# Layer 3's marks for experts: more of them at the MLPs' last products, at the attention's projections and at its first transposes

## The chip, the cores and the metric

The kernel runs on one core of a Trainium2 chip. The metric is the device time of one execution in microseconds (us), the median of several runs. TensorE is called PE, VectorE DVE, ScalarE ACT, GpSimd POOL and SyncE SP, as in the profile.

## The reference

The reference is a chain of four layers on x, 8 sequences of 256 tokens with 128 features, all in float32. Each layer is a macaron: half a feed-forward part, an attention part, half a feed-forward part again, each behind a layer norm and added to x. Only layer 3 matters here:

```python
x = x + 0.5 * _L3_ffn_ref(_layernorm(x), ...)
x = x + _L3_attn_ref(_layernorm(x), ...)
x = x + 0.5 * _L3_ffn_ref(_layernorm(x), ...)

def _L3_ffn_ref(x, ...):            # attention within a sequence, then eight dense experts
    x = x + softmax(q k^T * scale) v @ Wo + bo
    gates = softmax(x @ Wg + bg)
    hmid = relu(einsum('bsh,ehd->bsed', x, W1) + b1)      # 8 experts, 128 -> 512
    eout = einsum('bsed,edh->bseh', hmid, W2) + b2        # 512 -> 128
    return x + einsum('bse,bseh->bsh', gates, eout)

def _L3_attn_ref(x, ...):
    xm = mix(x); n = rms_norm(xm)
    value, gate = split(n @ in_proj)                      # causal convolution, silu
    Bm, Cm = xm @ B_proj, xm @ C_proj
    xm = xm + scale * ((scan(value, Bm, Cm) + D * value) * silu(gate) @ out_proj)
    xm = xm + scale * (relu(rms_norm(xm) @ fc)**2 @ proj)     # MLP "m"
    xa = mix(xm, x); n = rms_norm(xa)
    q, k, v = n @ q_w, n @ k_w, n @ v_w                   # 16 heads of 8, 4 of k and v; norms, rope
    xa = xa + scale * (softmax(causal q k^T) v @ o_w)
    return xa + scale * (relu(rms_norm(xa) @ a_fc)**2 @ a_proj)   # MLP "a"
```

## The kernel before

Tokens lie on the 128 partitions; x stays in SBUF as 16 tiles of 128 tokens by 128 features. After layer 0 the kernel works in two halves, `a` and `b`, of four sequences (1024 tokens) each. The stages of a half are numbered 0 to 11; layer 3 is 9 (`l3_ffn`), 10 (`l3_attn`) and 11 (`l3_ffn` again). `run` writes out an order in which a stage of one half is built beside the experts of the other: the experts of (b, 9) beside stage (a, 10), those of (a, 11) beside (b, 10), those of (b, 11) alone at the end.

An expert part is a loop over eight experts `e` and two groups `g` of 512 tokens (`l3_ffn`, lines 1595 to 1620). For each it makes four `ph` products (L1600), relu with bias into `hT` (three on ACT, L1608, the fourth on DVE, L1606), sixteen `po` products (L1612) and four updates of `x_res` on DVE (L1618). The weights of an expert come by `experts` (L943), in turn from SP's and ACT's queue, into three buffers; so a load waits for the expert three before it.

A scheduler of the framework sets the order of instructions on each engine; each engine then runs its queue in order. What ties the experts to the other half are marks. `step(inst, weight)` appends an instruction of the stage to a list, `weight` times. `keep_pace` picks for every `ph` an entry of that list and makes a dependency without a semaphore: the scheduler puts the `ph` behind that instruction, and nothing waits for it on the chip.

```python
    def step(self, inst, weight=1):
        self.steps += [inst.ins] * weight
    def keep_pace(self, inst, part):
        if self.pace:
            mark = self.pace[int(part * self.share * (self.marks or len(self.pace)))]
```

`part` is (2 * e + g) / 16. `share` is 0.8 (`EARLY`) for (b, 9) and 1.0 for (a, 11). So the place of a `ph` depends on the whole length of the list and on where its entries lie.

The marks of one stage 10 before, in the order of the list:

- `l3_scan`, the scan of four batches (sequences): 16 in each, at the products `sc` (L1752). A batch begins with `pv` (L1712), a convolution on DVE (L766, L768) and silu on ACT, transposes `pvt` (L1720), the gate `pg` (L1730), then `pbc` (L1746), `sc`, `y` (L1766), and ends with `yT` on DVE and POOL (L1772, L1775) and `po` (L1779).
- `l3_mlp` "m": `rms` (L1629 to L1635: square on ACT, sum, root on ACT, reciprocal L238, scaling L1634, transposes L231), then for two groups four `ph` (L1659, a mark each), relu on ACT, square on POOL and DVE (L1665), sixteen `po` (L1669): 8 marks.
- `blend` (L1867 to L1871), and in `l3_gqa` the setup (`attn_setup`: casts, four issues on ACT L544), `rms` and the projections `qkv` (L1802, 2 marks each): 16 marks.
- `attn_batches`: for each of four batches `prepare` (rotations on DVE and POOL, L1840 to L1845), `attn_stack` (a split of q and k in three bf16 parts, L573 to L576, 24 transposes `tpb` L593 in eight groups of three, evictions `sT`, and a trip through DRAM: `l_parts` L600 from SP for q and from ACT for k, then `qs` and `ks` L601 from SP), one batch later the maxima (`attn_max`, L617 to L621) and three later the mixing (`attn_mix`, L653 to L700). Maxima and mixing have 8 marks per batch each: 64.
- `l3_mlp` "a": 8 marks.

Together 160.

Of the kernel before, what the change touches and what calls it, by code (L numbers as in the profile page):

```python
# [19 lines left out]
NT = T // P  # L20
# [145 lines left out]
class Chip:  # L166
# [411 lines left out]
    def attn_stack(self, a, b, q, k, pool, psum):  # L578


        nc = self.nc
        kv = a["kv"]
        n = 8 * kv
        sT = pool.tile([P, 2, 3, S], BF16, name="sT", tag="sT")
        qs = pool.tile([75, 16, S], BF16, name="qs", tag="qs", bufs=4)
        ks = a["ks"][b % 4]
        for side, (x, m, h, dst) in enumerate(((q, P, 16, qs), (k, n, kv, ks))):
            sp = pool.tile([P, 3, 2, m], BF16, name=f"sp{side}", tag=f"sp{side}")
            self.split3(pool, x, [sp[:, i] for i in range(3)], f"sp{side}")
            for t in range(2):  # L590
                ps = psum.tile([P, 3, P], BF16, name="tpb", tag="m")
                for i in range(3):
                    nc.tensor.transpose(ps[0:m, i, :], sp[:, i, t, :], a["ident_b"])  # L593
                at = (1 - t if side == 0 else t) * P
                self.evict(sT[0:m, side, :, at : at + P], ps[0:m])

            dr = self.tc.dram_tile([3, 3, m, S], BF16, name=f"l_parts{side}")
            for i in range(3):
                out = (dr[i], dr[:, i])[side]
                (nc.sync, nc.scalar)[side].dma_start(out.rearrange("s r t -> r s t"), sT[0:m, side])  # L600
            nc.sync.dma_start(  # L601
                dst[0:72].rearrange("r h t -> r (h t)"), dr.rearrange("i s (d h) t -> (i s d) (h t)", h=h)
            )
        return qs
# [272 lines left out]
class Half(Chip):  # L877
# [768 lines left out]
    def l3_mlp(self, xm, n, scale):  # L1646

        nc = self.nc
        with ExitStack() as ctx:
            pool = ctx.enter_context(self.sb("l3m"))  # L1650
            fc, proj = self.load(pool, f"l3a_{n}fc"), self.scaled(pool, f"{n}proj", scale)
            wk = ctx.enter_context(self.sb("l3mw", 2))
            psum = ctx.enter_context(self.ps("l3mps", 2))
            nT = self.rms(pool, psum, xm, "h")
            for g in range(self.T // 512):
                hT = wk.tile([P, 4, 512], F32, name="hT", tag="hT")
                for k in range(4):
                    ps = psum.tile([P, 512], F32, name="ph", tag="h")
                    mm = nc.tensor.matmul(  # L1659
                        ps, fc[:, k * P : (k + 1) * P], nT[:, 512 * g : 512 * g + 512], start=True, stop=True  # L1660
                    )
                    self.step(mm)
                    nc.scalar.activation(hT[:, k, :], ps, AF.Relu)
                    eng = (nc.gpsimd, nc.vector)[k % 2]
                    eng.tensor_tensor(hT[:, k, :], hT[:, k, :], hT[:, k, :], ALU.mult)  # L1665
                po = psum.tile([P, 4, D], F32, name="po", tag="o")
                for i in range(4):
                    for k in range(4):
                        nc.tensor.matmul(  # L1669
                            po[:, i, :], hT[:, k, i * P : (i + 1) * P], proj[:, k, :], start=(k == 0), stop=(k == 3)  # L1670
                        )
                xs = xm[:, 4 * g : 4 * g + 4, :]
                nc.vector.tensor_tensor(xs, xs, po, ALU.add)

# [110 lines left out]
    def l3_gqa(self, xa):  # L1785

        nc, NT = self.nc, self.NT
        with ExitStack() as ctx:
# [4 lines left out]
            a = self.attn_setup(one, 4, 1)  # L1793
# [3 lines left out]
            with self.sb("l3gn") as np_:  # L1797
                nT = self.rms(np_, psum, xa, "m")
                for g in range(0, NT, 2):
                    ps = psum.tile([P, 2, 192], F32, name="qkv", tag="m")  # L1800
                    for i in range(2):
                        mm = nc.tensor.matmul(  # L1802
                            ps[:, i, :], nT[:, (g + i) * P : (g + i + 1) * P], w["qkv"], start=True, stop=True
                        )
                        self.step(mm, 2)
                    self.evict(qk[:, g : g + 2], ps[:, :, 0:160])
                    nc.scalar.copy(v[:, g : g + 2].rearrange("p t h d -> p t (h d)"), ps[:, :, 160:192])
            part = lambda z, k: (z[:, :, 0:P], z[:, :, P:160])[k].rearrange("p t (d h) -> p t d h", d=8)
# [97 lines left out]
```

## Time and profile before

| | before |
|---|---|
| median of 5 runs | 2828.45 us (2823.78 to 2832.7) |
| the profiled execution, time | 2824.83 us |
| the profiled execution, span from first to last instruction | 2823.0 us |
| mean granted PE clock | 0.889 |
| PE / DVE / ACT / POOL busy | 83% / 57% / 36% / 11% |

The page of the profile lists the busy time of every engine, groups of instructions by line with their mean time, and the chain of work that ended last. Further views are cut to a stretch of time: a table of stretches (busy time, granted PE clock, share of DMA), a timeline of one engine (start, length, line, what is written from what, and in brackets the idle time before it with what ended it) and the waits. A float32 product shows as two rows, one for each of its two passes; a bf16 product as one.

In the profiled execution the scan's four batches of half a end at 1822.4, 1866.6, 1909.7 and 1952.9 us, those of half b at 2274.2, 2318.3, 2360.4 and 2406.4 (starts of L1779).

### The profile page before, as it was taken

The page shows a single profiled execution, that of the slowest core. Times are in us where ns is not written, and L with a number is a line of the kernel's source. Part 1 is how long each engine was busy: PE and PEld are TensorE (multiplying, and loading weights), DVE is VectorE, ACT ScalarE, POOL GpSimd, SP SyncE. Part 2 cuts the span into 40 slices and gives each one's busy share as a digit, 9 for nine tenths or more (in the row PEclk, how much of TensorE's full clock was granted, in tenths as well). Part 3 has the DMA queues.
Part 4 walks back from the last instruction along what each step waited for, and adds up shares of the span by engine and source line. Part 5 has one row for each costly group of instructions (what it writes and reads, how often), then busy time and mean ns, then how long its engine had stood idle before and what let it go on. Part 6 is the DMA issues. An engine that isn't in the chain of part 4 may idle for free. (4 is left out here: it accounts for less than half of the span.)

```text
span 2823.0 us, 42755 instructions
## 1 busy us (share of the span) xinstructions
PE 2334.3 (83%) x17346; PEld 1544.9 (55%) x17346; DVE 1597.6 (57%) x3704; ACT 1027.3 (36%) x1754; POOL 319.5 (11%) x441
## 2 busy tenths in 40 slices
PE   5794788579689979878797898999698798779999
PEld 3672455367454535545465555666455565546666
DVE  6536442753458888788558746444644643453422
ACT  1021333212349669335453335212235321223322
POOL 0372110037000000000000000001201000210000
PEclk8695889669799989979998899899899899889999
DMA  7134321513200000110011001000211000030100
GB/s 259 21 42 108 104 79 45 208 22 41 79 19 17 16 23 23 32 30 24 7 40 32 17 16 50 1 16 17 68 47 38 27 8 16 26 93 3 43 23 23
DMA packets 103027, 127.27 MB, mean 45 GB/s; under 512 B 15161, under 2 KB 84094, under 8 KB 97726
## 3 DMA queue, kind: packets, MB, share of 16 engines
q1 hardware_dynamic: 61706, 71.56, 8.6%
q10 hardware_dynamic: 28836, 43.28, 4.6%
q0 software_dynamic: 12288, 9.71, 2.5%
q8 instruction: 136, 2.23, 0.3%
q14 instruction: 61, 0.50, 0.1%
HBM read 96.84 MB, written 27.53 MB: 44 GB/s over the span
## 5 line engine op out<-in xcount | busy, mean ns | idle before, releaser
L1612 PEld LDWEIGHTS po<-w_e,hT 128*128 128x128 f32 x2048 | 260.6, 195 | 69.6 <-issue 43.9
L1612 PE MATMUL po<-w_e,hT 128*128 128x128 f32 x2048 | 283.3, 283 | 12.0 <-DVE hT L1606 7.7
L1600 PE MATMUL ph<-x2T,w_e 128*128 128x512 f32 x512 | 267.1, 625 | 7.0 <-ACT hT L1608 6.3
L1608 ACT ACTIVATE hT<-ph,w_l_cols 128x512 f32<-128x512 f32 x192 | 131.5, 686 | 310.0 <-PE ph L1600 306.1
L621 DVE TENSOR_REDUCE nm<-sc 128x3 f32<-128x384 f32 (+1 forms) x192 | 130.5, 689 | 127.6 <-PE sc L619 126.4
L1040 PEld LDWEIGHTS po<-w_e,hT 128*128 128x128 f32 x1024 | 136.1, 199 | 80.0 <-DVE hT L1033 34.5
L658 ACT ACTIVATE pr_e<-scT 128x384 f32<-128x384 f32 (+1 forms) x192 | 111.3, 597 | 171.0 <-PE scT L655 161.1
L1040 PE MATMUL po<-w_e,hT 128*128 128x128 f32 x1024 | 146.0, 287 | 17.4 <-DVE hT L1033 13.3
L1030 PE MATMUL pu<-xnT,w_e 128*128 128x512 f32 x256 | 136.3, 614 | 8.7 <-ACT gs L1032 8.7
L231 PE MATMUL tp<-c_ident,xn 128*128 128x128 f32 x208 | 53.6, 379 | 105.0 <-DVE xn L251 97.0
L1027 PE MATMUL pg<-xnT,w_e 128*128 128x512 f32 x256 | 136.0, 613 | 1.8 <-ACT gs L1032 1.1
L1618 DVE SCALAR_TENSOR_TENSOR x_res<-po,gt,x_res 128x128 f32<-128x128 f32 x256 | 80.0, 358 | 86.3 <-PE po L1612 85.8
L500 ACT ACTIVATE gs<-pg 128x512 f32<-128x512 f32 x64 | 38.2, 597 | 248.7 <-PE pg L495 231.8
L1600 PEld LDWEIGHTS ph<-x2T,w_e 128*128 128x128 f32 x512 | 84.8, 195 | 69.9 <-ACT hT L1608 35.4
L1033 DVE SCALAR_TENSOR_TENSOR hT<-pu,w_l_bias,gs 128x512 f32<-128x512 f32 x128 | 94.7, 744 | 48.2 <-PE pu L1030 46.5
L1032 ACT ACTIVATE gs<-pg,w_l_bias 128x512 f32<-128x512 f32 x128 | 87.2, 688 | 86.5 <-PE pg L1027 78.8
L668 PE MATMUL ctx<-pr_e,vz 128*32 128x256 f32 x512 | 107.3, 397 | 2.8 <-ACT pr_e L658 2.8
L1758 DVE TENSOR_TENSOR gw<-sc,dec 128x768 f32<-128x768 f32 x64 | 61.2, 957 | 82.8 <-PE sc L1752 82.3
L513 POOL DMA_INDIRECT l_acc<-eo,idx x64 | 101.9, 1592 | 33.9 <-issue 16.3
L231 PEld LDWEIGHTS tp<-c_ident,xn 128*128 128x128 f32 x208 | 34.0, 171 | 125.5 <-DVE xn L251 82.0
L617 PE MATMUL sc<-ks,qs 72*128 72x256 bf16 x256 | 76.2, 298 | 28.3 <-DMA ks<-l_parts 17.5
L1046 ACT ACTIVATE ys<-po,pr 128x128 f32<-128x128 f32 x256 | 73.3, 368 | 63.9 <-PE po L1040 63.2
(604 smaller groups left out, 4991.5 us busy)
## 6 DMA issues: line engine op xcount, KB each, us to landing
l_parts<-sT SPq DMA_DIRECT2D x48, 192.0 KB, 5.2
qs<-l_parts SPq DMA_DIRECT2D x16, 576.0 KB
w_l_wu<-in_l_wu ACTq DMA_DIRECT2D x8, 1024.0 KB
w_e<-in_l_e SPq DMA_DIRECT2D x16, 512.0 KB, 3.6
w_e<-in_l_e ACTq DMA_DIRECT2D x16, 512.0 KB, 4.2
w_e<-in_l_e SPq DMA_DIRECT2D x16, 384.0 KB, 3.3
w_e<-in_l_e ACTq DMA_DIRECT2D x16, 384.0 KB, 3.0
l_parts<-sT ACTq DMA_DIRECT2D x24, 192.0 KB, 4.2
```

The costliest lines, as they stand in the source:

```text
L231: self.held(self.nc.tensor.transpose(ps[:, i * P : (i + 1) * P], src_of(g + i), self.ident), "tensor")
L513: nc.gpsimd.indirect_dma_start(out=accs[h][:, :], out_offset=bass.IndirectOffsetOnAxis(ap=idx[:, j : j + 1], axis=0), in_=eo[:, h, :], in_ ...
L621: nc.vector.tensor_reduce(blocks[:, hp * pr : hp * pr + hp, :], sc[:, :, 0:384].rearrange("p h (k t) -> p h k t", t=P), AX.X, ALU.max, neg ...
L658: nc.scalar.activation(pe, sc[:, :, 0:384], AF.Exp, scale=float(1.0 / np.sqrt(np.float32(8.0))))
L668: nc.tensor.matmul(o, z, pe[:, 0:S], start=(j == 0), stop=False)
L1027: mm = nc.tensor.matmul(pg, wg[:, c], xnT[:, cols], start=True, stop=True)
L1030: self.keep_pace(nc.tensor.matmul(pu, wu[:, c], xnT[:, cols], start=True, stop=True), part)
L1033: nc.vector.scalar_tensor_tensor(hT[:, k, :], pu, w["l1_bias"][:, 1, e, k : k + 1], gs, ALU.add, ALU.mult)
L1040: nc.tensor.matmul(po[:, i, :], hT[:, k, i * P : (i + 1) * P], wd[:, k * P : (k + 1) * P], start=(k == 0), stop=(k == 1),)
L1600: mm = nc.tensor.matmul(ps, we[:, k * P : (k + 1) * P], xnew[:, 512 * g : 512 * g + 512], start=True, stop=True)
L1608: nc.scalar.activation(hT[:, k, :], ps, AF.Relu, bias=bias)
L1612: nc.tensor.matmul(po[:, i, :], hT[:, k, i * P : (i + 1) * P], we[:, (4 + k) * P : (5 + k) * P], start=(k == 0), stop=(k == 3),)
```

## The change

Three places add marks. In `attn_stack` the last transpose of each group of three counts three times, for the first two batches. In `l3_mlp` the last `po` of the last group counts eight times. In `l3_gqa` each projection counts three times instead of two, and the last one six times more. Nothing is computed otherwise. `l3_mlp` runs twice in a stage, so its eight marks come twice. The list grows from 160 to 214 entries: 64 of the scan, 16 of the first MLP, 30 of the projections, 24 of the first two batches' transposes, 64 of maxima and mixing, 16 of the second MLP. `attn_stack` also serves layer 0, where `step` does nothing.

```diff
@@ -590,7 +590,10 @@
             for t in range(2):
                 ps = psum.tile([P, 3, P], BF16, name="tpb", tag="m")
                 for i in range(3):
-                    nc.tensor.transpose(ps[0:m, i, :], sp[:, i, t, :], a["ident_b"])
+                    mm = nc.tensor.transpose(ps[0:m, i, :], sp[:, i, t, :], a["ident_b"])
+                if b < 2:
+
+                    self.step(mm, 3)
                 at = (1 - t if side == 0 else t) * P
                 self.evict(sT[0:m, side, :, at : at + P], ps[0:m])
 
@@ -1666,9 +1669,12 @@
                 po = psum.tile([P, 4, D], F32, name="po", tag="o")
                 for i in range(4):
                     for k in range(4):
-                        nc.tensor.matmul(
+                        mm = nc.tensor.matmul(
                             po[:, i, :], hT[:, k, i * P : (i + 1) * P], proj[:, k, :], start=(k == 0), stop=(k == 3)
                         )
+                if g == self.T // 512 - 1:
+
+                    self.step(mm, 8)
                 xs = xm[:, 4 * g : 4 * g + 4, :]
                 nc.vector.tensor_tensor(xs, xs, po, ALU.add)
 
@@ -1802,7 +1808,9 @@
                         mm = nc.tensor.matmul(
                             ps[:, i, :], nT[:, (g + i) * P : (g + i + 1) * P], w["qkv"], start=True, stop=True
                         )
-                        self.step(mm, 2)
+                        self.step(mm, 3)
+                    if g == NT - 2:
+                        self.step(mm, 6)
                     self.evict(qk[:, g : g + 2], ps[:, :, 0:160])
                     nc.scalar.copy(v[:, g : g + 2].rearrange("p t h d -> p t (h d)"), ps[:, :, 160:192])
```

## The prediction

> **What bounds the kernel now.** I read the page's head first, then stretches cut at the stage limits that the TensorE (PE) timeline shows, then the waits and the chain inside them. The head:
>
> ```profile
> PE 2334.3 (83%) x17346; PEld 1544.9 (55%) x17346; DVE 1597.6 (57%) x3704; ACT 1027.3 (36%) x1754; POOL 319.5 (11%) x441
> ```
>
> PE is busy for 83%, so what matters is where its other 17% lie. The change acts from about 1800 us on, in the two attention stages of layer 3: half a (1800 to 2196) and half b (2230 to 2658). Beside each the experts of the other half are the filling. I call the four `ph` products (L1600) and sixteen `po` products (L1612) of one expert and one group a unit. Each product has two rows in the trace (two passes): six `ph` rows from 1978.62 to 1981.39 give 0.92 us for one product, 26 `po` rows from 2009.96 to 2012.86 give 0.223 us, so a unit is 4 x 0.92 + 16 x 0.223 = 7.3 us of PE.
>
> Stretches of PE alone (start:end, length, busy, rows, granted clock, DMA share, GB/s):
>
> ```profile
> 1866.60:1909.70 43.10, 40.08 (x260) 1.00 0.04 13
> ...
> 2360.40:2406.40 46.00, 38.82 (x229) 0.85 0.04 14
> 1953.90:1965.20 11.30, 10.66 (x52) 1.00 0.01 1
> 2166.10:2179.10 13.00, 7.63 (x18) 0.61 0.59 195
> 1978.60:1996.80 18.20, 6.79 (x40) 0.81 0.14 36
> 1996.80:2007.60 10.80, 9.32 (x31) 0.68 0.00 1
> 2007.60:2035.60 28.00, 18.42 (x100) 0.76 0.33 90
> 2035.60:2048.70 13.10, 13.07 (x100) 1.00 0.28 75
> 2432.00:2450.20 18.20, 6.81 (x40) 0.83 0.25 70
> 2450.20:2463.10 12.90, 9.91 (x26) 0.50 0.01 1
> 2463.10:2490.80 27.70, 11.56 (x64) 0.68 0.28 73
> 2490.80:2506.70 15.90, 15.67 (x92) 0.76 0.21 59
> ```
>
> The first two are one batch of the scan each. The first holds two units and is 43.1 long; the second (half b, fourth batch) holds little over one and is 46.0 long: less work, more time. Its head says why (PE timeline: start, length, what, idle before and its end):
>
> ```profile
> 2362.04 1.13 PE L1712 MATMUL pv<-rmsT,w_l3a_in 128*128 128x256 f32 x4
> 2367.47 1.35 PE L1720 MATMUL pvt<-c_ident,vT 128*128 128x128 f32 x4 [4.30 <-DVE vT L768]
> 2369.74 2.07 PE L1730 MATMUL pg<-rmsT,w_l3a_in 128*128 128x256 f32 x4 [0.92 <-ACT vz L223]
> ```
>
> The head waits for VectorE's (DVE's) convolution whether a unit stands there or not. With one, the clock stays at 1.00 and `pg` takes 1.13; without, it falls to half and `pg` takes 2.07. So a unit in a head is free, and its absence costs. The third and fourth rows compare the start of an MLP behind a covered and an uncovered norm in the same way: 11.3 against 13.0. The other rows are the gaps that the change aims at: blend and norm (18.2, of which PE is busy 6.8), the projections, the stack's bf16 transposes with their trip through DRAM, and the first maxima.
>
> **The change part by part.** It adds no work; it lengthens the list of marks from 160 to 214 entries per stage, and expert (e, g), n = 2e + g, is held behind entry n/16 x 0.8 x length (half a) or n/16 x length (half b). The instruction orders of both built programs show what comes of it. Up to the scan's end and the norm behind it half a ran units 0 to 7 and now runs 0 to 5; blend: 8, now 6 and 7; projections and stack: 9 and 10, now 8, 9 and 10 (less two `po`); the rest is as many as before. Half b: scan and norm 0 to 6, now 0 to 4; blend: 7, now 5; projections and stack: 8, now 6, 7 and 8. So in each half two units leave places where they were cover (the head of the third batch, the norm behind the scan), and two enter gaps. No unit leaves a stretch where PE is full: each batch keeps its unit in the middle, and the attention keeps five. This is why I expect little gain.
>
> Half a, step by step:
> - Head of the third batch uncovered. From `po` (L1779) to the first `sc`: 1866.59 to 1881.20, 14.6 covered; 2360.37 to 2377.49, 17.1 uncovered; one more slow `pbc` (1.34 for 1.13). **+2.7**. The `ph` that stood ahead of L1779 in the second and fourth batch leaves too, for nothing: L1779 waits for POOL's `yT` there (0.54 idle at 1952.88).
> - Norm behind the scan uncovered: 13.0 for 11.3, +1.7; two `po` fewer in the MLP, -0.45. **+1.25**, bounds 0.75 (a wait of 0.5 for POOL's square swallows part) to 1.7.
> - Blend. The added unit 7 fits: PE waited 10.2 us for DVE's `rmsn` up to 1996.81. But DVE and ACT are queues too. Its `hT` (L1606, 0.72) goes ahead of the sum L1630, which is hidden, because `rms_s` on ACT came only at 1995.90, behind the four issues of L544. Its four L1618 (1.13 together) go ahead of the reciprocal L238 at 1996.14, with everything of the norm behind them, and they wait for the unit's last `po`. PE can begin those only after that `hT` (about 1993.4), thirteen `po` of 0.223 end at 1996.3 to 1997.8 (full or half clock), so L238 moves to 1997.5 to 1999.1 and the transposes by 1.6 to 3.0 us. Against that stands the clock: from 1996.8 to 2003.5 PE ran at 0.50; at full clock two transposed groups, one `qkv` and one `ph` save 0.49 + 0.51 + 0.83 + 0.93 = 2.8 at most. I take **+0.5**, bounds -0.9 and +3.0, nearer the middle because the gaps left are about 3.5 and 1.9 us.
> - Stack. Nearly one more unit: four `ph` now stand among the first transposes, three `hT` (0.69 each) among ACT's casts, evictions and the `l_parts` issue, one L1606 and four L1618 on DVE. The chain goes POOL `ro`, ACT and DVE split, PE, eviction, ACT issue (2026.64), landing, SP's `ks` (2029.75), 2035.58. ACT was busy 4.0 of the 7.3 us up to its issue, PE waited 0.4 to 0.6 before each group. At full clock a `ph` overlaps an eviction and I find the issue 0.3 later; at half clock (1.7 for a `ph`, as at 2460.3) 2.2 later. **+0.8**, bounds 0 and +2.2. The loads of experts move too: on SP behind the small constants (half a) or ahead of the second batch's `ks` (half b), which would wait with it, on ACT behind `l_parts`. Each waits for a unit whose last `po` stands ahead of it on PE by several us, so nothing: 0; if it did wait, `ks` of the second batch would come late, and with it the bound of 2.2.
> - First maxima: the two `po` left over, **+0.45**.
>
> Sum for half a: 2.7 + 1.25 + 0.5 + 0.8 + 0.45 = +5.7.
>
> Half b:
> - Scan. In the second batch nine `po` no longer stand ahead of the last `y` (PE is full there): -2.0. Head of the third uncovered: +2.7. The fourth was uncovered already. **+0.7**.
> - Norm and MLP: **+1.25**. Blend: still one unit, **0**.
> - Projections: half a, with a `ph` between them, shows 10.8 where b has 12.9: **-2.1**. Stack: 28.0 in half a with one unit more than b's 27.7, +0.3, and the +0.8 of above: **+1.1**.
> - First maxima: 15.9 at clock 0.76 become half a's 13.1 at 1.00, and the two `po`: -2.8 + 0.45 = **-2.35**, bounds -2.8 and +0.45.
> - Rest of the attention and the second MLP: the same seven units, but some sixteen `po` (3.6) move from the end into the mixing, where PE is full, and the last norm loses part of its cover; against that the maxima of the second batch, which wait for DVE and DMA, take nine `po` for nothing. **-0.5**, bounds -2.0 and +3.6.
>
> Sum for half b: 0.7 + 1.25 - 2.1 + 1.1 - 2.35 - 0.5 = -1.9. Together **+3.8 us**, or 0.13%. The profiled execution had a span of 2823.0 and a time of 2824.83, and would become 2828.6; its time lies 3.6 under the median of the runs, and I add the sum to the median: 2828.45 + 3.8 = 2832.25.
>
> [...] Granted clock around one short wait:
>
> ```profile
> 2061.40:2063.50 2.10, 0.07 (x2) 1.00 0.35 82
> 2063.50:2064.90 1.40, 1.12 (x12) 1.00 0.00 0
> 2064.90:2068.70 3.80, 3.80 (x16) 0.55 0.59 161
> 2068.70:2071.00 2.30, 2.30 (x14) 1.00 0.03 9
> ```
>
> A wait of 2.1 us brings, 1.4 us later, a half clock for 3.8 us; so I don't count the short gaps that the added unit leaves in the blend as warm. [...]
>
> **The rivals.** (1) Faster. The warm clock is worth more: from 1996.8 half a could gain by its two more units what b lacks against a today (12.9 + 27.7 + 15.9 = 56.5 against 10.8 + 28.0 + 13.1 = 51.9, so 4.6). Then a is 2.7 + 1.25 - 4.6 = -0.65; b, without the delay in the stack and with its best end, 0.7 + 1.25 - 2.1 + 0.3 - 2.8 - 2.0 = -4.65: -5.3 together, 2823; a little more if the norm costs less. For it: clocks of 0.68 and 0.76 in those rows. Against: half a's stack is 28.0 with one unit more than b's 27.7, so it is a chain, not PE. That the scan gives back the units' 7.3 us each would be more, but the batch of 46.0 us speaks against it. (2) Slower. The filling stands ahead of the chain on PE, ACT and DVE: L238 behind four L1618 (+3.0), `l_parts` 2.2 later in each half, the sixteen `po` in full (+3.6). Half a: 2.7 + 1.25 + 3.0 + 2.2 + 0.45 = 9.6; b: 0.7 + 1.25 - 2.1 + 2.5 - 2.35 + 3.6 = 3.6; +13, 2841.6. It decides once the transposes of half a's projections begin more than 2 us later after the MLP than now (18.2). For it: in-order queues whose waits I know. Against: DVE and ACT have idle time in both gaps. (3) That nothing moves is excluded by the orders.
>
> **How the numbers follow.** About 0.2% (5.65 us) is what a measurement of this kernel can tell from no change. The forecast's own sum goes with its bounds to both sides of +5.65: within 0.2% 0.47 (2822.8 to 2834.1). Rival 1, and what goes beyond it, 0.17 faster; rival 2 and the upper part of the forecast 0.36 slower. The range reaches from rival 1 with 1 us more (2822) to rival 2 (2842) and leaves about a tenth out at each end; all low bounds of the forecast together give only -2, but the five runs before lie 4.5 us to either side of their median.
>
> **What the profile after would show.** Right: PE waits over 4 us ahead of `pvt` in one more batch per half, with `pg` near 2.07; a clock near 0.6 behind the scan's norm; half b's projections near 10.8 and its first maxima near 13.1; half a's blend 18 to 21. Wrong: batches with an uncovered head of 43 or less; a stack well over 30, or well under 27; half a shorter from 1800 to 2196, or half b longer.

## The result and the profile after

| | before | after |
|---|---|---|
| median | 2829.19 us (60 runs) | 2836.93 us (33 runs) |
| ratio of the times | | 1.0029, 95% interval 1.0021 to 1.0036 |
| the profiled execution, time and span | 2824.83 and 2823.0 us | 2833.47 and 2831.7 us |

The change makes the kernel slower by 8 us. That lies inside the predicted range, but beyond the 0.2% within which the forecast had put it, on the slower side. Lines behind the edits move: L1600, L1612, L1618 and L1779 are now L1603, L1615, L1621 and L1785.

The head of the page:

```profile
PE 2348.8 (83%) x17346; PEld 1548.2 (55%) x17346; DVE 1598.7 (56%) x3704; ACT 1026.9 (36%) x1754; POOL 319.1 (11%) x441
```

The same 17346 rows (instructions, two of them for a float32 product) keep PE busy for 14.5 us longer, while the span grows by 8.7: idle time was filled, but part of what that won is lost again in rows that now run at half clock (0.50 granted, `pg` at 2.07 us for 1.13), as the lines below show. Where, the stretches of PE alone show (start:end, length, busy, rows, granted clock, DMA share, GB/s), in the order third batch of half a, fourth of half b, norm behind half a's scan, then blend, projections, stack and first maxima of half a, and the same four of half b:

```profile
1866.60:1913.20 46.60, 38.86 (x223) 0.85 0.02 3
2375.90:2421.90 46.00, 38.14 (x226) 0.85 0.08 25
1958.60:1970.20 11.60, 7.45 (x19) 0.71 0.07 30
1983.00:2004.50 21.50, 15.75 (x79) 0.92 0.16 36
2004.50:2016.00 11.50, 9.74 (x31) 0.70 0.10 36
2016.00:2046.80 30.80, 25.48 (x136) 0.83 0.24 64
2046.80:2060.20 13.40, 13.40 (x106) 1.00 0.41 117
2447.40:2465.40 18.00, 6.61 (x39) 0.84 0.26 71
2465.40:2476.90 11.50, 10.03 (x31) 0.66 0.01 1
2476.90:2507.70 30.80, 25.63 (x135) 0.83 0.23 60
2507.70:2521.10 13.40, 13.40 (x103) 1.00 0.43 125
```

PE's busy time in half a's blend rises from 6.8 to 15.8 us and in its stack from 18.4 to 25.5: the units are where the change sends them. Yet both stretches became longer (18.2 to 21.5, 28.0 to 30.8), and so did the batch that lost its unit (43.1 to 46.6). The head of that batch in the PE timeline:

```profile
1868.24 1.13 PE L1718 MATMUL pv<-rmsT,w_l3a_in 128*128 128x256 f32 x4 [0.51 <-DVE xm L1789]
1873.53 1.35 PE L1726 MATMUL pvt<-c_ident,vT 128*128 128x128 f32 x4 [4.16 <-DVE vT L771]
1875.80 2.07 PE L1736 MATMUL pg<-rmsT,w_l3a_in 128*128 128x256 f32 x4 [0.92 <-ACT vz L223]
```

It is the picture that half b's fourth batch showed before: 4.2 us of waiting, then `pg` at 2.07 instead of 1.13. The same `pg` before, behind a unit:

```profile
1876.28 1.13 PE L1730 MATMUL pg<-rmsT,w_l3a_in 128*128 128x256 f32 x4
```

Half a's blend, from DVE's, ACT's and PE's timelines (start, length, what, idle before and its end):

```profile
1994.71 2.39 DVE L536 CAST ident_b<-c_ident 128x128 bf16<-128x128 f32 x1
1994.98 2.30 DVE L1621 SCALAR_TENSOR_TENSOR x_res<-po,gt,x_res 128x128 f32<-128x128 f32 x1
1997.20 0.74 DVE L1609 TENSOR_SCALAR hT<-ph,w_l_cols 128x512 f32<-128x512 f32 x1
1999.31 0.17 DVE L236 TENSOR_SCALAR rms_s<-rmsm 128x8 f32<-128x8 f32 x1
2001.15 0.21 ACT L237 ACTIVATE rms_s<-rms_s 128x8 f32<-128x8 f32 x1 [5.53 <-DMA ks<-one]
2002.83 1.12 DVE L1621 SCALAR_TENSOR_TENSOR x_res<-po,gt,x_res 128x128 f32<-128x128 f32 x4 [3.35 <-PE po L1615]
2003.87 0.19 DVE L238 RECIPROCAL rms_s<-rms_s 128x8 f32<-128x8 f32 x1
...
1997.99 4.80 PE L1615 MATMUL po<-w_e,hT 128*128 128x128 f32 x26 [3.69 <-DVE hT L1609]
2004.53 0.63 PE L231 MATMUL tp<-c_ident,rmsn 128*128 128x128 f32 x3 [1.74 <-DVE rmsn L1637]
```

And the end of the same blend before:

```profile
1990.23 2.40 DVE L536 CAST ident_b<-c_ident 128x128 bf16<-128x128 f32 x1
1995.90 0.21 ACT L237 ACTIVATE rms_s<-rms_s 128x8 f32<-128x8 f32 x1 [4.75 <-DMA ks<-one]
1996.14 0.20 DVE L238 RECIPROCAL rms_s<-rms_s 128x8 f32<-128x8 f32 x1 [1.57 <-ACT rms_s L237]
1996.81 1.09 PE L231 MATMUL tp<-c_ident,rmsn 128*128 128x128 f32 x4 [10.21 <-DVE rmsn L1634]
```

The second unit's fourth relu (L1609) stands on DVE behind a cast that takes 2.39 us. Its `po` wait 3.69 us for it and then run at half clock for most of their time (0.50 granted from 1998.85 to 2002.26; 4.80 us for 26 rows, where the first unit's took 3.17 at 1.00). Its four updates of x wait for them, and L238, whose root was ready at 2001.4, comes behind the updates at 2003.87; before, it followed its root at once. That is 2.5 of the 3.5 us. The other 1.0 is the root itself: counted from the end of the MLP's last `po` it begins at 18.1 us, before at 17.1, behind ACT's four issues of L544, which take 3.96 us instead of 3.19.

The stack, from PE's timeline:

```profile
2030.84 2.07 PE L1603 MATMUL ph<-x2T,w_e 128*128 128x512 f32 x2
2032.70 0.53 PE L593 MATMUL tpb<-ident_b,sp 128*128 128x128 bf16 x3
2033.69 2.08 PE L1603 MATMUL ph<-x2T,w_e 128*128 128x512 f32 x2 [0.46 <-ACT hT L1611]
2035.69 0.50 PE L593 MATMUL tpb<-ident_b,sp 128*32 128x128 bf16 x3
2036.63 0.48 PE L593 MATMUL tpb<-ident_b,sp 128*32 128x128 bf16 x3 [0.44 <-DVE sT L221]
2037.04 2.08 PE L1603 MATMUL ph<-x2T,w_e 128*128 128x512 f32 x2
```

A `ph` takes 2.07 here (the granted clock from 2030.8 to 2039.0 was 0.50), and a group of three transposes waits for each. Before, two such groups followed each other after 1.05 us:

```profile
2023.66 0.48 PE L593 MATMUL tpb<-ident_b,sp 128*128 128x128 bf16 x3 [0.59 <-DVE sT L221]
2024.71 0.48 PE L593 MATMUL tpb<-ident_b,sp 128*32 128x128 bf16 x3 [0.57 <-ACT sT L223]
```

### The profile page after: what moved, and what is told of

The parts are those of the page before. It is cut to its first block, busy times and chain, and to the rows that moved or that the text cites. A ratio compares the mean times of both kernels' runs of the same rounds, so it can differ in the third digit from the quotient of the medians.

```text
span 2831.7 us, 42759 instructions
## 1 busy us (share of the span) xinstructions
PE 2348.8 (83%) x17346; PEld 1548.2 (55%) x17346; DVE 1598.7 (56%) x3704; ACT 1026.9 (36%) x1754; POOL 319.1 (11%) x441
## 5 line engine op out<-in xcount | busy, mean ns | idle before, releaser
L1615 PEld LDWEIGHTS po<-w_e,hT 128*128 128x128 f32 x2048 | 259.6, 196 | 64.1 <-issue 39.5
L1615 PE MATMUL po<-w_e,hT 128*128 128x128 f32 x2048 | 280.9, 284 | 11.1 <-DVE hT L1609 6.9
L1603 PE MATMUL ph<-x2T,w_e 128*128 128x512 f32 x512 | 271.5, 633 | 7.0 <-ACT hT L1611 6.3
L1621 DVE SCALAR_TENSOR_TENSOR x_res<-po,gt,x_res 128x128 f32<-128x128 f32 x256 | 80.6, 357 | 100.0 <-PE po L1615 99.8
L1603 PEld LDWEIGHTS ph<-x2T,w_e 128*128 128x128 f32 x512 | 84.6, 196 | 71.2 <-ACT hT L1611 36.6
L513 POOL DMA_INDIRECT l_acc<-eo,idx x64 | 101.9, 1592 | 32.6 <-issue 16.4
## 6 DMA issues: line engine op xcount, KB each, us to landing
w_l_wu<-in_l_wu ACTq DMA_DIRECT2D x8, 1024.0 KB, 18.4
```

The costliest lines, as they stand in the source:

```text
L513: nc.gpsimd.indirect_dma_start(out=accs[h][:, :], out_offset=bass.IndirectOffsetOnAxis(ap=idx[:, j : j + 1], axis=0), in_=eo[:, h, :], in_ ...
L1603: mm = nc.tensor.matmul(ps, we[:, k * P : (k + 1) * P], xnew[:, 512 * g : 512 * g + 512], start=True, stop=True)
L1615: nc.tensor.matmul(po[:, i, :], hT[:, k, i * P : (i + 1) * P], we[:, (4 + k) * P : (5 + k) * P], start=(k == 0), stop=(k == 3),)
```

## The experiments

**The theory** (of the places): the 8 us come from places. A lost head costs 3 to 4 us, the second unit of the blend 3.4 by the queue shown above, a unit in the stack 3. **Rivals**: the added work itself lengthens the gaps, whatever the queues; or the loss sits in one of the three marks; or it is the heads alone, and what enters the gaps balances out.

Lengths, in us, are read between landmarks in the PE timeline of each profiled run, so they don't depend on where the run stood when layer 3 began: the first L1779 of half a came between 1813 and 1830 us. Batches run from L1779 to L1779, the blend from the end of the MLP's last `po` to the transposes behind it (the stretches of before are cut up to 0.2 earlier, hence 18.2 where the table has 18.0), the stack from the projections' end to the first `sc`, the end of half b from the second MLP's first `ph` to L1507, the last of the next stage's first products (`pvo`). A star marks a batch whose head no unit covers, (2) a blend that holds the `ph` of two units. Where the text gives the gain or loss of a whole run in us, it is the ratio less 1, times 2828; the ratio is not exactly that of the medians.

| run | ratio, 95% interval | third a | fourth a | third b | fourth b | blend a | blend b | stack a | stack b | end b |
|---|---|---|---|---|---|---|---|---|---|---|
| before | | 43.1 | 43.2 | 42.1 | 46.0* | 18.0 | 18.0 | 27.8 | 27.5 | 24.5 |
| after | 1.0029 (1.0021, 1.0036) | 46.6* | 44.3 | 46.3* | 46.1* | 21.5 (2) | 18.0 | 30.7 | 30.8 | 25.1 |
| e1 | 1.0032 (1.0016, 1.0049) | 42.9 | 42.9 | 45.8* | 42.1 | 21.5 (2) | 21.3 (2) | 26.5 | 27.3 | 25.0 |
| e2 | 0.9984 (0.9969, 1.0000) | 42.9 | 42.9 | 47.1* | 42.1 | 18.0 | 18.0 | 29.8 | 30.6 | 21.6 |
| e3 | 0.9974 (0.9958, 0.9990) | 42.9 | 42.1 | 48.3* | 43.5 | 18.0 | 18.0 | 29.1 | 29.6 | 19.9 |
| e4 | 0.9986 (0.9971, 1.0000) | 43.1 | 43.2 | 43.5 | 45.5* | 17.9 (2) | 18.0 | 29.7 | 29.3 | 25.1 |
| e5 | 1.0043 (1.0027, 1.0058) | 42.1 | 46.4* | 46.7* | 46.0* | 18.0 | 17.5 | 33.4 | 30.8 | 20.6 |
| e6 | 0.9997 (0.9982, 1.0011) | 46.7* | 44.3 | 45.1* | 48.3* | 19.0 (2) | 18.0 | 33.6 | 30.6 | 25.2 |
| e7 | 0.9991 (0.9979, 1.0002) | 43.2 | 44.6 | 43.5 | 45.5* | 16.4 | 16.4 | 28.1 | 27.5 | 24.5 |
| e8 | 0.9952 (0.9937, 0.9967) | 43.5 | 43.7 | 43.5 | 42.9 | 18.3 | 18.0 | 31.0 | 29.0 | 16.8 |
| e9 | 0.9951 (0.9939, 0.9964) | 45.0 | 42.8 | 43.2 | 44.6 | 18.3 | 18.0 | 27.3 | 27.0 | 20.2 |
| e10 | 1.0038 (1.0025, 1.0051) | 46.6* | 44.3 | 46.3* | 46.1* | 18.0 | 17.0 | 27.5 | 27.2 | 28.3 |
| e11 | 0.9966 (0.9949, 0.9982) | 43.1 | 43.2 | 42.1 | 46.6* | 18.0 | 16.0 | 28.1 | 27.3 | 24.5 |
| e12 | 0.9903 (0.9875, 0.9931) | 45.0 | 42.8 | 42.1 | 42.9 | 17.1 | 16.4 | 27.3 | 30.3 | 16.8 |

The lengths are those of one execution per kernel, and the table doesn't hold everything. The stretch between the halves, from half a's L1507 to half b's first L1779, holds four `ph` and ten `po` in every kernel and yet is 65.5 (e9) to 75.3 us (e10) long, 71.1 before and after. In e9 the scheduler orders the start of the next stage differently, in e10 PE waits 3.6 us in it; why was not followed up.

**e1 to e3: one mark each.** e1 keeps of the diff only the eight marks at the MLP's last `po`, e2 only the projections', e3 only the transposes'.

> Only the mark at the MLP's last product is added. By the instruction order half a keeps its scan and its norm as before; one unit moves from the projections into the blend, which then holds two units as after the full change. Half b: head of the third batch uncovered, head of the fourth covered (it was not before), the norm uncovered, two units in the blend. Theory of the queues (the second unit's four L1618 stand ahead of L238): half a's blend, from the MLP's last product to the next transposes, is 21 to 22 us as in the changed kernel (18.2 before), and half b's too (18.2 before); with +4.2 and -3.0 for the two heads of half b the whole is about +8 us, 1.0028. Rival (the blend grew in the changed kernel because the stretch began with a PE slowed to half clock, not because of the second unit): blends near 18.5 and the whole near +1.5 us.

Measured +9 us (1.0032), blends of 21.5 and 21.3. As the theory of the queues had it, the blend with the second unit is about 3.4 longer in both halves; half b's lost head (+3.7) and gained one (-3.9) cancel.

> Only the marks at the projections are added. By the instruction order half a keeps scan, norm and blend as before; five `ph` stand between the first transposes and the first maxima (none before), and the maxima and mixing hold four `ph` and three `po` fewer (4.3 us of PE). Half b: third head uncovered, fourth covered, norm uncovered, two units instead of one between qkv and the first maxima plus four `ph` there, and four `ph` and fourteen `po` fewer behind (6.8 us). If a unit among the first transposes holds up the chain, half a's stretch from the projections' end to the first `sc` is 30 to 31 us (28.0 before); if not, 28. If maxima and mixing are bound by PE, they give back the units that left: half a +2.9 - 4.3 = -1.4, half b +4.2 - 3.0 + 0.2 - 1.1 + 3.0 - 2.5 - 6.8 = -6.0, together -7 us, 0.9974. If they are bound by their own chain, nothing comes back and the whole is near +4 us, 1.0013.

Measured 0.9984, -4.5 us, between the two. The stacks are 29.8 and 30.6: units there do hold up the chain. Half b's mixing (from the end of the first maxima to the end of the last L700) got 1.8 shorter, its end 2.9.

> Only the marks at the first transposes are added. By the instruction order half a's scan is as before, its norm behind the scan is uncovered, five `ph` stand in the stack, and the attention holds as much as before (thirteen `po` more). Half b: third head uncovered, fourth covered, norm uncovered, six `ph` in the stack. Expected by the prices read from the changed kernel: norm +0.2, stack +2.9, `po` +2 in half a; heads +1.2, norm +0.2, stack +3.0, maxima -2.5, two `ph` fewer -1.8 in half b: about +5 us, 1.0018. If the norm costs what the prediction gave it (+1.25 each), +7 us. If units in the stack cost nothing, -1 us.

A miss: expected +5, measured -7.4 us (0.9974), though the stacks are longer (29.1, 29.6) and half b's third batch (48.3) too. What I had not counted is the last column: half b's end fell from 24.5 to 19.9, with no `ph` left in it, and its mixing (119.2 to 114.7). From e1 to e3 it looked as if the MLP's mark were the whole loss; e5 tests that.

**e4: the scan's weight.** The whole change, and at L1752 (the mark of `sc`):

```diff
-                    self.step(mm, 2)
+                    self.step(mm, 3)
```

> The whole change, and the scan's marks weighted 3 for 2 (96 marks for 64), so that the scan and the norm behind it hold their units as before in both halves, while blend, projections and stack of half a keep their two more units, half b its one. Eight `ph` and seventeen `po` (11.2 us of PE) leave maxima and mixing of half a, seven `ph` and sixteen `po` (10 us) those of half b. Theory 1 (the attention behind the first maxima is bound by PE): half a +3.4 (blend) + 2.9 (stack) - 11.2 = -4.9, half b -1.1 + 3.0 - 2.5 - 10 = -10.6; together -15 us, 0.995. Theory 2 (it is bound by its own chain, and only order in the queues counts): +6.3 - 0.6 = +6 us, 1.002. Batches of 43 to 44 us in half a's third and half b's third would show that the lost cover lengthened them in the changed kernel (46.6 and 46.3).

Measured -4 us (0.9986), between both. With their heads covered half a's third batch is back at 43.1, half b's at 43.5. The eight `ph` that left half a's mixing brought nothing: 118.9 us against 117.5, and for 16 us of it (2127 to 2143) PE ran at a clock of 0.72. One length is a surprise: two units in half a's blend, in the order of e1, and 17.9 us. Its lines:

```profile
1989.60 0.42 DVE L536 CAST ident_b<-c_ident 128x128 bf16<-128x128 f32 x1
1990.12 0.74 DVE L1609 TENSOR_SCALAR hT<-ph,w_l_cols 128x512 f32<-128x512 f32 x1
1994.12 1.12 DVE L1621 SCALAR_TENSOR_TENSOR x_res<-po,gt,x_res 128x128 f32<-128x128 f32 x4 [1.73 <-PE po L1615]
...
1990.92 3.17 PE L1615 MATMUL po<-w_e,hT 128*128 128x128 f32 x26 [1.72 <-DVE hT L1609]
```

The cast took 0.42 instead of 2.39. So the relu is 2.0 us earlier, the `po` wait 1.72 instead of 3.69, keep their pace (3.17 us for 26 rows, as the first unit's at 1.00), and against before's 18.0 the price of 3.4 is gone. But before's blend holds the long cast too. A blend with one unit and a cast of 0.42 is on record in e11's half b, and it is 16.0 us long, with L238 right behind its root (with the long cast the blends of both halves are equal, 18.0):

```profile
2440.83 0.42 DVE L536 CAST ident_b<-c_ident 128x128 bf16<-128x128 f32 x1
2444.73 0.20 DVE L238 RECIPROCAL rms_s<-rms_s 128x8 f32<-128x8 f32 x1 [0.63 <-ACT rms_s L237]
```

Like for like the second unit therefore costs 1.9 us beside a short cast and 3.4 beside a long one. The wait behind the cast explains the difference; the rest, a root about 1.0 later and 0.9 for L238 behind the four updates, comes with the unit in either case. So the rival, that the added work itself lengthens the gap, is not excluded: part of the price stays without the long cast.

**e5: the change without the MLP's mark.** The diff without its second hunk.

> The change without the mark at the MLP's last product. By the instruction order half a's blend holds one unit again, its third head is covered, its fourth is not, the norm is covered; half b's third and fourth heads are uncovered, its norm is covered, its blend holds no unit; projections and stack hold as much as in the changed kernel; the end of half b's stage has no `ph` left. Theory (the whole loss came with that mark; the other two marks are worth what they gave alone, 0.9984 and 0.9974): between 0.996 and 0.9985, blend 18.0 in half a. Rival 1 (the terms of the stages add up: half a +2.9 for the fourth head, +2.9 for the stack; half b +4.2 +3.3 -2.5 -1.6): about +9 us, 1.003. Rival 2 (the marks only disturb each other): 1.000.

The theory that the loss came with that mark falls: 1.0043, +12 us, nearest to rival 1, which had +9 from the sum of the stages. Taking the mark out shortens the list, and in half a the head of the fourth batch loses its unit instead of the third (46.4); the stack is at 33.4.

**e6: the relu.** The whole change, and in `l3_ffn`:

```diff
-                        if k % 4 == 3:
+                        if k % 4 == 3 and not (self.pace and self.share < 1 and 2 * e + g == 7):
```

> The whole change; only the fourth relu of the second unit in half a's blend (one instruction of 128x512) is made by ACT instead of DVE. In the instruction order the unit's four x updates then stand behind the norm's scaling on DVE and six of its sixteen `po` behind the blend's transposes. Theory of the queue (the relu waits on DVE behind the cast of L536, so the `po` wait 3.7 us, run at half clock, and hold L238 behind the four updates): half a's blend goes from 21.5 back to 18.0 to 18.7, and the whole from 1.0029 to about 1.0018. Rival (the second unit's work itself lengthens the blend): it stays at 21 to 22.

The blend went to 19.0, a little over the theory's 18.7: L238 follows its root at once again, and what is left over 18.0 is the root, which begins 18.1 us after the MLP's end as in the changed kernel. But the rest of the unit now stands behind it, and the stack grew to 33.6: from the first L1779 to the end of the stage half a took 392.5 us, the changed kernel 392.8. The whole nevertheless came out at 0.9997. The condition also held for one unit of half a's first expert part, before 1800 us, and e11 shows what that did.

**e7: the cast.** The kernel before, and in `attn_setup`:

```diff
-        nc.vector.tensor_copy(a["ident_b"], self.ident)
+        if kv_heads == 4:
+            nc.scalar.copy(a["ident_b"], self.ident)
+        else:
+            nc.vector.tensor_copy(a["ident_b"], self.ident)
```

> The kernel before; only the cast of the identity to bf16 in layer 3's setup (L536, 128x128) is made by ACT instead of DVE. Theory: on DVE this cast waits about 2 us while POOL runs its back-to-back memsets of 128x1024 (2.40 us in every blend measured but one, where it took 0.42), and L540, L1618 and the sum L1630 wait behind it; without it both blends shrink from 18.0 to about 16.0 us and the whole by about 4 us, 0.9986. Rival 1 (the root on ACT behind the four issues of L544 is bound by something else): 18.0 and no change. Rival 2 (ACT's queue pays for the cast): blends of 18.3 and slightly slower.

Both blends fell to 16.4, 1.6 of the expected 2.0. On the whole, 0.9991 (0.9979 to 1.0002), no gain is established.

**e8 and e9: the scan's weight without the MLP's mark, and alone.** e8 is e5 with the edit of e4; e9 is the kernel before with the edit of e4 and nothing else.

> The marks of projections and transposes, no mark at the MLP, and the scan's marks weighted 3 for 2. By the instruction order every head of the scan in both halves is covered, half b's fourth too; each blend holds one unit; projections and stack hold two units; maxima and mixing hold a third fewer `ph` than before. Compared with the run that had the same weights and the MLP's mark too (0.9986): half b's fourth head covered, 46.0 to 43 us, so -3: 0.9976. If covered heads are worth more than that, 0.995; if units that leave the mixing let PE's clock fall there (0.72 for 16 us in that run), no better than 0.9986.

> The kernel before with one edit: the scan's marks weighted 3 for 2, and none of the change's three marks. By the instruction order every head of the scan in both halves is covered, half b's fourth too; half a's blend holds the rest of two units, its projections two units, its stack no `ph`, half b's blend one, its projections one, its stack none; four `ph` remain behind the second MLP's start where before there were more. Theory 1 (units in heads pay 3 to 4 us each, units in the stack cost 1.5 to 3): against the run with the scan's weight and two of the change's marks (0.9952) the stacks come back from 31.0 and 29.0 to 27.8 and 27.5, so -18 us, 0.9935. Theory 2 (what paid in that run were the two marks in the gaps): only half b's fourth head remains, -3 to -4 us, 0.9987.

Both are 14 us faster than before (0.9952, 0.9951), more than the heads explain. e8 came out where its expectation had put heads worth more than 3 us, but by luck: against e4 its fourth head in half b saves 2.6, while the mixing there is 5.0 and the end 8.3 shorter. For e9 -18 was expected and -14 came: its stacks are back at 27.3 and 27.0, 3.7 and 2.0 shorter than e8's, but its end of half b is 20.2 against 16.8. So the two marks in the gaps, beside a scan that keeps its units, are worth nothing on balance. Against before, e9's profile is 10.2 us shorter in half b from its first L1779 to L1507 (374.4 for 384.6; of this the mixing 4.5, the end 4.3), 5.6 shorter in the stretch between the halves, and 2.1 longer in half a (382.7 for 380.6). Only one head is gained (half b's fourth, 1.4); most of the gain lies elsewhere. At the end of half b fewer units are left; in the mixing and between the halves nearly the same ones stand as before, and no run separates why these are shorter. The end of half b in the stretches of PE alone, of before, e10, e9 and e8:

```profile
2634.27:2658.77 24.50, 23.41 (x137) 1.00 0.23 77
2641.40:2669.70 28.30, 27.39 (x150) 1.00 0.20 67
2632.40:2652.50 20.10, 16.58 (x94) 1.00 0.18 50
2631.50:2648.30 16.80, 15.79 (x84) 1.00 0.19 49
```

By the orders this stretch holds 3 `ph` and 22 `po` before, 7 and 25 in e10, 0 and 4 in e9, none in e8. From e8 to before that is 3 x 0.92 + 22 x 0.223 = 7.7 us of units, and the stretch is 7.7 longer: as long as units stand there, PE is busy for 23.4 of 24.5 us and a unit costs its full time. The changed kernel has 4 and 16 there and 25.1 us: it took hardly any of this away. e9 is the exception. Its four `po` are worth 0.9 us, and it is 3.4 longer than e8, because there PE waits for the weights of the next stage:

```profile
2651.72 0.46 PE L1505 MATMUL pvo<-w_l_in 128*128 128x128 f32 x2 [2.61 <-DMA w_l_in<-in_l_in]
```

**e10: the heads alone.** The kernel before, with the changed kernel's entries for the units of the scan and each later unit at the entry that the next one had, in `keep_pace`:

```diff
-            mark = self.pace[int(part * self.share * (self.marks or len(self.pace)))]
+            n, at = int(16 * part), int(part * self.share * (self.marks or len(self.pace)))
+            if len(self.pace) == 160:
+                early, k = (((0, 10, 21, 32, 42, 53), 8), ((0, 13, 26, 40, 53), 10))[self.share == 1.0]
+                at = early[n] if n < len(early) else min(k * (n + 1), 159)
+            mark = self.pace[at]
```

> The kernel before; the marks that the units take in the scan are the changed kernel's (entries 0, 10, 21, 32, 42, 53 in half a, 0, 13, 26, 40, 53 in half b), and each later unit takes the mark that the unit after it had before. By the instruction order the head of the third batch is uncovered in both halves as in the changed kernel, the norm, the blend, the projections and the stack hold what they held before, and one unit more per half stands behind the attention's mixing. Theory of the heads: the third batches become 46.6 and 46.3 us (43.1 and 42.1 before), +3.4 and +4.2, and the unit that moved costs 0 to 5 us in each half where it now stands: +8 to +17, 1.003 to 1.006. Rival (a lost head is made up behind it): 1.000.

Measured +10.7 us (1.0038), with the third batches at 46.6 and 46.3 and nothing of the change's filling in blend and stack. The two stretches read as in the changed kernel:

```profile
1867.10:1913.70 46.60, 38.86 (x222) 0.85 0.01 2
2326.80:2373.10 46.30, 38.94 (x227) 0.85 0.00 1
```

In its profile the scans of both halves are together 7.7 us longer (half a's second, third and fourth batches -0.2, +3.5 and +1.2, half b's -1.0, +4.2 and +0.1), and the end of half b 3.8, because the unit from the head now stands there. Its other stretches move too: the one between the halves is 4.2 longer, the rest of half b behind its scan together 5.6 shorter. So uncovering these heads, with the units pushed behind, is enough for a loss as large as the whole one. Whether the units in the gaps give some of it back is not shown: by the ratios the changed kernel is 2.5 us faster than e10, but the two intervals overlap, and in its profile the stretches behind the scan are longer on balance.

**e11: the early relu.** The kernel before, and in `l3_ffn`:

```diff
-                        if k % 4 == 3:
+                        if k % 4 == 3 and not (self.tag == "a" and self.share < 1 and 2 * e + g == 7):
```

> The kernel before; the fourth relu of one unit (expert 3, group 1) of half a's first expert part, which runs beside half b's stage before, is made by ACT instead of DVE: the second edit that the run with the relu on ACT contained unintentionally. If that instruction is why that run came out at 0.9997 while its stages from 1800 us on were as long as the changed kernel's (392.5 and 384.8 us from the first to the last landmark of each half), the time up to the first batch of the scan is 8 to 10 us shorter than in other kernels: 0.997. If the shorter start was chance: 1.000.

Measured 0.9966, -9.6 us: the gain of e6 came from here, not from the blend. One relu on another engine (0.69 us on ACT) does not save that itself. By the orders it makes the scheduler place the last unit of that expert part earlier: behind the products of L1476, with which half b's stage there ends, four `ph` and sixteen `po` fewer are left, one unit of 7.3 us. From the last of these products to the next stage's first one the profiles show 41.6 us before, 35.7 in e11 and 33.5 in e6. Why the scheduler does so was not followed up.

**e12: what paid, together.** On the kernel before: the scan's weight (e4's edit) in both halves, the marks at projections and first transposes in half b alone, the cast of e7, the relu of e11.

> Everything that paid, on the kernel before: the scan's marks weighted 3 for 2 in both halves; the marks at projections and first transposes in half b alone; no mark at the MLP; the cast of L536 on ACT; the fourth relu of that one early unit on ACT. If the stages add up: half a as in the run with the scan's weight alone (382.7 us from its first to its last landmark, less 2.0 for the blend), half b as in the run with the scan's weight and two marks (367.0, less 2.0), together -4 - 19.5 against before's 380.6 and 384.6 (the blends' share in it), and -9.6 for the early relu measured alone: 0.9885 to 0.991. If the early relu and the cast gain nothing beside the marks: 0.995.

Measured 2797.97 us against 2828.63 in the runs of before beside it, 0.9903. Half a's stage took 379.6 us from the first to the last landmark and half b's 365.4 (before 380.6 and 384.6), and half a's first L1779 came at 1812.9, 9.5 us earlier; in the kernels without the early relu it came between 1821.6 and 1829.9. What each part adds beside the others this run doesn't show.

## Why the prediction was right and wrong

The sum pointed to a loss, and a loss it is, but of 8 us where it gave 3.8: the likeliest case, within 0.2%, did not come. By the profile the terms come out so (from the first L1779 of a half to L1507 half a takes 392.8 for 380.6 us and half b 383.7 for 384.6):

| term | half a forecast | measured | half b forecast | measured |
|---|---|---|---|---|
| scan | +2.7 | +4.4 | +0.7 | +3.3 |
| norm and MLP | +1.25 | -0.35 | +1.25 | -0.4 |
| blend and projections | +0.5 | +4.0 | -2.1 | -1.6 |
| stack | +0.8 | +2.9 | +1.1 | +3.3 |
| first maxima | +0.45 | +0.3 | -2.35 | -2.5 |
| rest | 0 | +0.9 | -0.5 | -3.0 |
| sum | +5.7 | +12.2 | -1.9 | -0.9 |

The two halves together are 11.3 us longer, three times the forecast sum. The last stage behind them took 2.7 less, with nothing changed there; in the other profiles it is up to 4.0 shorter and 4.7 longer than before, so this is scatter, and the profiled pair's difference of 8.7 holds a gain that the change can't claim. The sum of half a is less than half of what was measured; that the time still lies in the range is owed to its upper end, which is rival 2's, and not to the sum.

- **Heads.** Right in mechanism, too small (+2.7; measured +3.5 in half a's third batch and +4.2 in half b's). 19 batches with an uncovered head measure 46.4 on average (45.1 to 48.3), 37 with a covered one 43.2 (42.1 to 45.0): 3.2 us. The +2.7 was read up to the first `sc`; the rest of the batch adds to it. And the `ph` that left ahead of L1779, "for nothing", left the fourth batch of half a 1.2 longer; e10 shows the same 44.3 with the heads alone.
- **Norm.** Wrong in sign. The 13.0 us of an uncovered norm were read at the norm behind the attention; behind the scan the same stretch measures 11.6 without a unit (third line of the stretches above) and 11.3 with one. Without it the first `ph` comes 1.5 us sooner after the scan's last L1779 (7.2 for 8.7), and the MLP takes 1.2 longer (18.4 for 17.2). Cover that has to be worked off ahead of the chain is no gain.
- **Blend.** The delay it reckoned, 1.6 to 3.0, was nearly the answer for the blend (3.4), and the value taken, 0.5, was not. The relu was placed right: forecast at 1993.4, measured 14.9 us after the MLP's end, 1993.7 on the clock of before. That the relu ahead of the sum L1630 is hidden held; but the root, behind ACT's issues, came 1.0 later, which no term had. Wrong above all was to set up to 2.8 of warmer clock against the delay. PE waited 3.69 us for that relu, the clock fell 0.9 us after the `po` had begun, and projections 0.6 longer, not shorter, followed.
- **Stack.** The reading at half clock, which was kept as the bound of 2.2 and not taken, is what happened: 2.07 for a `ph`; the stacks, 2.9 and 3.3 longer, went beyond that bound. In the runs half b's stack goes with what stands in it by the orders from its first transpose on: nothing 27.0 to 27.5 us, three `ph` and sixteen `po` 29.0 to 30.3, six and sixteen 29.6, four and 27 30.6 to 30.8.
- **First maxima, projections of half b, its blend.** As forecast (-2.5, -1.6, 0).
- **Rest of half b.** Beyond its bound of -2.0: the mixing is 2.4 shorter, the norm behind it 1.2, the end 0.6 longer. Nearly the same units stand there (in mixing and norm 20 `ph` and 81 `po` for 21 and 79), and no run separates the cause.

Rival 2 was to decide once half a's transposes begin more than 2 us later after the MLP: they do (21.5 for 18.2), and half a's blend and stack are what it said or more (+4.0 and +2.9 for 3.0 and 2.2). The cost of 3.6 that it gave the sixteen `po` of half b did not come. Of the prediction's own signs, half a's blend lies just outside the 18 to 21 that were to show it right. The likeliest case failed at one choice, made twice: between a bound by the queue and a bound by the clock it took the middle, though no row showed the clock recover in such a gap.

On the clock: behind e4's wait of 1.72 us the 26 rows of `po` took 3.17, as the changed kernel's first unit did at a granted clock of 1.00. Behind the changed kernel's 3.69 us the clock was 0.50 from 1998.85 to 2002.26, then 1.00 up to 2005.68; behind the wait of 2.1 shown before it was 0.50 from 2065.07 to 2068.49. These three stretches are 3.4 us long each. What it is in a wait that brings the clock down, no run here tests. The gap that decided was not the 1.9 us reckoned ahead of the transposes but the one ahead of the `po`.

What stays open: the profile of e7 gives back in other stretches the 3.2 us that its blends won and 1.3 more, and its runs don't tell whether any of it is lasting.

## What to carry to other kernels

When filling is placed by shares of a list, a mark added in one place takes filling from all others: write down for each unit where it leaves, and ask first whether PE was covered there. In these runs a unit paid its full time only where it left a stretch that PE itself bounds (the end of half b, 7.7 us for 7.7 us of units); moved from one wait to another it cost what it stood ahead of, on every queue that its parts use. Then the cheapest edit may be the opposite one: weighting the scan instead of the gaps, one character, made this kernel 0.5% faster.

## What was not expected of the hardware

A cast of 128x128 to bf16 on DVE (L536) took 2.39 to 2.66 us in most of the blends, 1.41 in one and 0.42 in two. Beside it POOL sets zeros in one stretch; in the changed kernel's POOL timeline:

```profile
1993.21 1.84 POOL L551 MEMSET vz<- 128x1024 f32 x2
1995.08 0.95 POOL L551 MEMSET vz<- 128x1024 f32 x1
1996.07 0.95 POOL L551 MEMSET vz<- 128x1024 f32 x1
```

The cast began at 1994.71 and ended at 1997.10, just behind the last of these (1997.02), and the update of x queued behind it (0.33 in e4) shows 2.30. Blends with one unit are 18.0 to 18.3 us with a cast of 2.4, 17.0 with 1.41 (e10), 16.0 with 0.42 (e11), and 16.4 with the cast on ACT (e7). The memset under way when the cast began ended at 1995.05, and the cast went on through two more. In e4 it began at the same distance, 1.40 us, from the start of L1879, which waits for POOL's part of the blend just ahead of the memsets, and it took 0.42. What holds the cast up, and why not in e4, no run here shows.
